# Attention heads of a graph-and-transformer kernel: another PSUM ring for the next pair's keys, longer pieces, and a fixed order on VectorE

## The chip, the cores and the metric

The kernel runs on one core of one Trainium2 chip. The metric is device time in microseconds (us) of one execution. A core has TensorE (PE in the profile; its weight loads are PEld), VectorE (DVE), ScalarE (ACT), GpSimd (POOL) and SyncE (SP), and 16 DMA engines. Each engine takes its own instructions in order and waits on semaphores for the others. Matrix products land in PSUM[...].

## The reference, cut to what matters

Everything is fp32. 1250 nodes with 768 features pass two graph attention layers, and then one transformer block: attention with 12 heads of 64, and a mixture of 8 experts. The change touches the attention of that block alone:

```python
qkv = (x @ Wqkv).reshape(B, T, 3, H, HD)
q, k, v = (qkv[:, :, 0], qkv[:, :, 1], qkv[:, :, 2])
scores = jnp.einsum('bqhd,bkhd->bhqk', q, k) * jnp.float32(HD) ** (-0.5)
attn = jax.nn.softmax(scores, axis=-1)
out = jnp.einsum('bhqk,bkhd->bqhd', attn, v).reshape(B, T, D)
```

with B = 1, T = 1250, H = 12, HD = 64.

## The kernel before

The heads are worked in six pairs (p), and the queries in three chunks of 417, 417 and 416 (k). One pair and chunk is a unit: 18 units, one after the other. The 1250 keys of a unit lie in ten tiles of 125 (j). Scores are held transposed, keys on the partitions and two heads beside each other, so that a tile is 125 x 834 (832 in the third chunk).

Work on a unit is spread over two rounds of the loop at line 737. While unit `u` has its weights and values computed, the scores of the unit after it, `nxt`, are computed.

- `scores(j)` (line 655) takes a tile `st` from the ring `pair_psum` (two buffers of two banks each), makes both heads' products (L659), copies them to `sT` on ScalarE (L662) and, from j = 1 on, takes the running maximum `most` over the tiles on VectorE (L668). For j = 1 the maximum reads the copy of tile 0 and `st` of tile 1.
- `top()` (L675, L677) transposes `most` into a `ptop` tile of the same ring and reduces it on VectorE to one maximum per query, `m`. `row()` (L684) spreads `m` over the partitions into the tile `mb`, which has one buffer.
- `weights(j)` subtracts `mb` from `sT` on VectorE (L689), takes the exponential on ScalarE (L690) and sums the tiles on GpSimd into `acc` (L695).
- `values(j)` multiplies the weights by the values into `pav` on PE (L703).
- `divide()` of the unit before turns `acc` into the sums `pz` on PE (L712), and takes the reciprocal (L718) and the product (L719) on VectorE.

Between these, PE makes the keys and queries of the next pair, `queries_keys` (line 607): a generator that yields after each product over 128 features. For each chunk there are six steps for the keys (`pk`) and six for the queries (`pq`); after the sixth ScalarE moves the result to `qk` (L625). `go(steps, n)` runs n steps. Twelve steps fall in each unit of the first five pairs; the sixth pair has no next one, so its three units have none. `pk` takes the buffer of `mb`; `pq` takes that of `pz`. The weights `wqk` are fetched by SP, once per pair, into a single buffer.

The order of instructions on PE is as the program writes it inside `tc.manual_schedule`. On the other engines a planner puts them in order by its own estimate of what is ready first. The loop of before, in short:

```python
go(steps, DC - 2)
if nxt is not None:
    nxt.scores(0)
u.row()
u.weights(0)
u.weights(1)
```

and then five double steps, each with two `scores`, two `weights` and two `values`, the first with one `scores`; two steps of the queries go into each of the first three.

Of the kernel before, what the change touches and what calls it, by code (L numbers as in the profile page):

```python
# [10 lines left out]
F32 = mybir.dt.float32  # L11
# [16 lines left out]
def gnn_ffn_kernel(  # L28
# [27 lines left out]
    P = 128  # L56
    T = 125
    NT = N // T
# [101 lines left out]
    with tc.tile_pool(name="cnt", bufs=1) as cpool:  # L160
# [52 lines left out]
        with tc.tile_pool(name="edge", bufs=1) as ep, \  # L213
# [54 lines left out]
            def find_rows():  # L268
                nc.vector.tensor_scalar(begun, nodes, head, None, ALU.is_gt)
                pk = epc.tile([P, 512], F32, tag="pc", name="pk")  # L270
                for t in range(NT):
                    nc.tensor.matmul(pk[:T, t:t + 1], begun[:, t * T:(t + 1) * T], oneb,
                                     start=True, stop=True)
                return pk
# [56 lines left out]
            with tc.manual_schedule(engines=fixed):  # L331
                pk = find_rows()
# [64 lines left out]
            with tc.manual_schedule(engines={mybir.EngineType.PE, mybir.EngineType.DVE}):  # L397
                for g in range(NP // PG):
# [11 lines left out]
                    u, q0 = divmod(g * PG, T)  # L410
# [175 lines left out]
    with tc.tile_pool(name="att", bufs=2) as ap, \  # L586
# [8 lines left out]
        def pair_psum(name):  # L595
            return aps.tile([P, 2, 512], F32, tag="s", name=name)
# [10 lines left out]
        def queries_keys(p):  # L607

            wqk = ap.tile([P, DC, 2, P], F32, tag="wqk", name="wqk", bufs=1)
            for i in (1, 0):  # L610
                nc.sync.dma_start(wqk[:, :, i, :], Wqkv[:, i * D + p * P:i * D + (p + 1) * P].rearrange(
                    "(c p) f -> p c f", p=P))
            qk = ap.tile([P, 2, N], F32, tag="qk", name="qk")
            yield qk
            for c0, w in CHUNKS:
                for i in (1, 0):
                    if i == 1:
                        pq = apm.tile([P, 2, 512], F32, tag="mb", name="pk")[:, 0, :]
                    else:
                        pq = apa.tile([P, 512], F32, tag="pz", name="pq")  # L620
                    for c in range(DC):
                        nc.tensor.matmul(pq[:, :w], wqk[:, c, i, :], yT[:, c, c0:c0 + w],  # L622
                                         start=(c == 0), stop=(c == DC - 1))
                        if c == DC - 1:
                            nc.scalar.mul(qk[:, i, c0:c0 + w], pq[:, :w], 1.0 if i == 1 else HD ** -0.5)  # L625
                        yield None

        def go(steps, n):
            for _ in range(n if steps is not None else 0):
                next(steps, None)  # L630
# [15 lines left out]
        class Unit:  # L646
# [67 lines left out]
            def divide(self):  # L714
# [4 lines left out]
                nc.vector.tensor_tensor(aT[:, self.p, self.c0:self.c0 + w], self.pav[:, :w], rz[:, :w], ALU.mult)  # L719

        steps = queries_keys(0)
        qks = [next(steps)]
        wp = load_big_weight(Wproj, "wp")
        BEFORE = 2
        with tc.manual_schedule(engines={mybir.EngineType.PE}):
# [4 lines left out]
            u = Unit(0, 0, qks[0])  # L730
# [5 lines left out]
        steps = last = None  # L736
        for n, (p, k) in enumerate(units):
            if k == 0:
                steps = None
                if p + 1 < DC:  # L740
                    steps = queries_keys(p + 1)
                    qks.append(next(steps))
            nxt = Unit(*units[n + 1], qks[units[n + 1][0]]) if n + 1 < len(units) else None
            u.ns = NT if nxt is not None else NS
            with tc.manual_schedule(engines={mybir.EngineType.PE}):

                go(steps, 2)
                u.top()
                if last is not None:
                    last.divide()  # L750
                go(steps, DC - 2)
                if nxt is not None:
                    nxt.scores(0)
                u.row()
                u.weights(0)
                u.weights(1)
                for j in range(0, NT, 2):
                    for i in range(2):
                        if nxt is not None and j + i > 0:
                            nxt.scores(j + i)  # L760
                    if j < 6:
                        go(steps, 2)
                    for i in range(2):
                        if j + i + 2 < NT:
                            u.weights(j + i + 2)
                    for i in range(2):
                        u.values(j + i)
            last, u = u, nxt
# [305 lines left out]
```

## Time and profile before

| what | value |
|---|---|
| median of 3 runs | 1541.51 us (1534.36 to 1543.46) |
| the profiled execution | 1542.12 us |
| its span, first to last instruction | 1540.3 us |
| first unit's first `ptop` to that of unit 17 | 691.4 to 1176.8 us |
| PE busy over the span | 1454.5 us (94%) |
| VectorE busy over the span | 797.8 us (52%) |
| ScalarE busy over the span | 597.6 us (39%) |

In a group line of the profile stand the line, the engine, the operation, the tiles written and read, the shapes and the count; then the busy time and the mean duration in ns of one; then the idle time of the engine before these instructions and what ended most of it. In a timeline line stand the start, the length, the engine, the line and operation, and in brackets the idle time before and its releaser. A product of fp32 appears as two matmuls in the count, so `st` of one tile is four (two heads).

### The profile page before, as it was taken

How to read it: one execution, taken by the hardware profiler on the slowest of the kernel's cores; microseconds unless marked ns; L12 is line 12 of the kernel's file. 1: busy time of each engine (PE TensorE's matmuls, PEld its weight loads, DVE VectorE, ACT ScalarE, POOL GpSimd, SP SyncE). 2: the span in 40 equal slices, each digit the busy share in tenths (PEclk: the TensorE clock that was granted, in tenths of full speed). 3: DMA queues.
4: the chain of work that ended last, by engine and by line, in shares of the span. 5: the costliest groups of instructions: out<-in, count | busy, mean ns of one | idle time of the engine just before them, and what ended most of it. 6: DMA issues, size and time to landing. Idle time of an engine off the chain costs nothing.

```text
span 1540.3 us, 15938 instructions
## 1 busy us (share of the span) xinstructions
PE 1454.5 (94%) x5981; PEld 782.3 (51%) x5981; DVE 797.8 (52%) x1285; ACT 597.6 (39%) x950; POOL 431.6 (28%) x287
## 2 busy tenths in 40 slices
PE   3889999999999999999999999999988997799998
PEld 2476655555555555553344444434333665466665
DVE  4698633205326740117877877877888665011111
ACT  3321503202414621215655655655656354212121
POOL 5300000000000002004764664664666222122222
PEclk9956999999999999999999999999999997899999
DMA  6200010000021118940000000000030333755644
GB/s 182 66 1 32 11 72 0 0 11 2 1 81 55 56 44 339 407 176 20 1 21 1 21 0 21 1 21 1 0 101 1 131 119 113 288 169 179 219 153 142
DMA packets 48847, 125.49 MB, mean 81 GB/s; under 512 B 6103, under 2 KB 22680, under 8 KB 48768
## 3 DMA queue, kind: packets, MB, share of 16 engines
q1 hardware_dynamic: 30540, 55.04, 10.8%
q0 software_dynamic: 12688, 57.10, 9.8%
q10 hardware_dynamic: 5540, 12.31, 2.7%
q8 instruction: 48, 0.79, 0.2%
q14 instruction: 31, 0.25, 0.1%
HBM read 71.30 MB, written 57.60 MB: 84 GB/s over the span
## 4 chain that ended last, share of the span: by engine, by line
PE 71%; DVE 9%; issue 8%; DMA 5%; ACT 4%; POOL 2%; POOLq 0%; SPq 0%; ACTq 0%; DVEq 0%
PE pagg L525 12%; PE ph L201 9%; PE st L659 8%; PE pav L703 7%; PE pk L622 5%; PE pv L638 5%; PE phe L988 5%; PE poe L997 5%; PE pq L622 4%; DMA xd<-yn,slot 2%; DVE sT L689 2%; PE pc L409 2%; PE pe L190 2%; PE po L846 2%; PE ptr L140 1%
## 5 line engine op out<-in xcount | busy, mean ns | idle before, releaser
L695 POOL TENSOR_TENSOR acc<-acc,sT 125x834 f32<-125x834 f32 (+1 forms) x139 | 272.9, 1963 | 10.9
L525 PE MATMUL pagg<-h,wt 125*125 125x385 f32 (+1 forms) x800 | 262.7, 486 | 0.4 <-DVE wt L518 0.4
L668 DVE TENSOR_TENSOR most<-most,st 125x834 f32<-125x834 f32 (+1 forms) x144 | 147.0, 1021 | 105.3 <-ACT sT L662 101.9
L525 PEld LDWEIGHTS pagg<-h,wt 125*125 125x125 f32 x800 | 147.5, 187 | 106.0 <-DVE wt L518 2.7
L689 DVE TENSOR_TENSOR sT<-sT,mb 125x834 f32<-125x834 f32 (+1 forms) x180 | 174.1, 1016 | 22.9 <-PE mb L684 22.9
L690 ACT ACTIVATE sT<-sT 125x834 f32<-125x834 f32 (+1 forms) x180 | 158.4, 900 | 49.8 <-DVE sT L689 49.4
L662 ACT COPY sT<-st 125x834 f32<-125x834 f32 (+1 forms) x180 | 151.5, 847 | 51.4 <-PE st L659 46.4
L659 PE MATMUL st<-qk 64*125 64x417 f32 (+1 forms) x720 | 164.5, 556 | 3.9 <-DVE most L668 3.8
L703 PE MATMUL pav<-sT,v 125*64 125x417 f32 (+1 forms) x720 | 151.1, 532 | 9.3 <-ACT sT L690 9.3
L600 POOL MEMSET zero<- 128x772 f32 x1 | 0.7, 741 | 519.2 <-PE ptr L140 519.2
L695 POOL TENSOR_TENSOR acc<-sT 125x834 f32<-125x834 f32 (+1 forms) x18 | 35.3, 1963 | 276.0 <-ACT sT L690 276.0
L659 PEld LDWEIGHTS st<-qk 64*125 64x125 f32 x720 | 56.6, 184 | 99.1 <-DVE most L668 42.9
L703 PEld LDWEIGHTS pav<-sT,v 125*64 125x64 f32 x720 | 42.5, 136 | 106.0 <-issue 44.5
L997 PE MATMUL poe<-we,hT 128*128 128x384 f32 x264 | 88.8, 486 | 0.0
L622 PE MATMUL pq<-yT,wqk 128*128 128x417 f32 (+1 forms) x216 | 88.1, 534 | 0.0
L846 PE MATMUL po<-wp,aT 128*125 128x384 f32 x240 | 87.5, 498 | 0.0
L988 PE MATMUL phe<-xT,we 128*128 128x384 f32 (+1 forms) x288 | 86.6, 460 | 0.0
L1001 DVE SCALAR_TENSOR_TENSOR sofar<-poe,weight,sofar 128x768 f32<-128x768 f32 x25 | 25.4, 1018 | 116.3 <-PE poe L997 116.2
L622 PE MATMUL pk<-yT,wqk 128*128 128x417 f32 (+1 forms) x216 | 84.0, 526 | 0.0
L201 PE MATMUL ph<-gw,xnT 128*125 128x384 f32 x240 | 82.6, 504 | 0.0
L638 PE MATMUL pv<-wv,yT 128*125 128x384 f32 x240 | 79.9, 490 | 1.4 <-issue 1.4
L201 PE MATMUL ph<-gw,x1T 128*125 128x384 f32 x240 | 78.6, 487 | 0.0
(219 smaller groups left out, 1734.6 us busy)
## 6 DMA issues: line engine op xcount, KB each, us to landing
xd<-zero POOLq DMA_DIRECT2D x8, 3860.0 KB, 47.4
we<-in_L_ffn_W_dram SPq DMA_DIRECT2D x16, 1152.0 KB
xr<-xd SPq DMA_DIRECT2D x25, 386.0 KB
gw<-in_L_gnn_W_dram SPq DMA_DIRECT2D x2, 2304.0 KB
wqk<-in_L_ffn_Wqkv_dram SPq DMA_DIRECT2D x12, 384.0 KB
xres<-in_x_dram SPq DMA_DIRECT2D x10, 375.0 KB
xsd<-xres ACTq DMA_DIRECT2D x10, 375.0 KB
wv<-in_L_ffn_Wqkv_dram SPq DMA_DIRECT2D x1, 2304.0 KB
```

The lines of the kernel that those rows point to most:

```text
L201: nc.tensor.matmul(po[:, s, :DH], xT[:, c, t * T:(t + 1) * T], w[:, c, s * DH:(s + 1) * DH], start=(c == 0), stop=(c == DC - 1))
L525: nc.tensor.matmul(po[:, s, :DH + s], ws[j][:, (d - d0) * T:(d - d0 + 1) * T], h[:, j, s * DH:(s + 1) * DH + s], start=(j == 0), stop=(j = ...
L622: nc.tensor.matmul(pq[:, :w], wqk[:, c, i, :], yT[:, c, c0:c0 + w], start=(c == 0), stop=(c == DC - 1))
L638: nc.tensor.matmul(pv[:T, s, :DH], yT[:, c, t * T:(t + 1) * T], wv[:, c, s * DH:(s + 1) * DH], start=(c == 0), stop=(c == DC - 1))
L659: nc.tensor.matmul(st[:T, i, :w], self.qk[r, 1, j * T:(j + 1) * T], self.qk[r, 0, self.c0:self.c0 + w], start=True, stop=True)
L662: nc.scalar.copy(s[:, :, :w], st[:T, :, :w])
L689: nc.vector.tensor_tensor(s[:, :, :w], s[:, :, :w], self.mb[:T, :, :w], ALU.subtract)
L690: nc.scalar.activation(s[:, :, :w], s[:, :, :w], AF.Exp)
L695: nc.gpsimd.tensor_tensor(self.acc[:, :, :w], prev[:, :, :w], s[:, :, :w], ALU.add)
L703: nc.tensor.matmul(self.pav[r, :w], v[:, j, hd0:hd0 + HD], s[:, i, :w], start=(j == 0), stop=(j == NT - 1))
L988: nc.tensor.matmul(ph[:, :n * P], w1[:, c, f * P:(f + 1) * P], xT[:, c, :n * P], start=(c == 0), stop=(c == DC - 1))
L997: nc.tensor.matmul(po[:, d, :DH], hT[:, f, s * P:(s + 1) * P], w2[:, f, d * DH:(d + 1) * DH], start=(f == 0), stop=(f == FC - 1))
```

## The change

Three things. The keys' tile `pk` comes from the scores' ring `pair_psum`, and no longer from the buffer of `mb`. VectorE's instructions in the loop are kept in the order of the program, as PE's are. And the order of the loop is another: `scores(0)` moves from before `row()` into the first double step; three `weights` stand ahead of the double steps and not two, and run three tiles ahead of `values`; the queries' six steps come as four right after these and two in the second double step, and no longer as three times two.

```diff
                 for i in (1, 0):
                     if i == 1:
-                        pq = apm.tile([P, 2, 512], F32, tag="mb", name="pk")[:, 0, :]
+                        pq = pair_psum("pk")[:, 0, :]
                     else:
                         pq = apa.tile([P, 512], F32, tag="pz", name="pq")
...
-            with tc.manual_schedule(engines={mybir.EngineType.PE}):
+            with tc.manual_schedule(engines={mybir.EngineType.PE, mybir.EngineType.DVE}):
 
                 go(steps, 2)
                 u.top()
                 if last is not None:
                     last.divide()
                 go(steps, DC - 2)
-                if nxt is not None:
-                    nxt.scores(0)
                 u.row()
-                u.weights(0)
-                u.weights(1)
+                for j in range(3):
+                    u.weights(j)
+                go(steps, 4)
                 for j in range(0, NT, 2):
                     for i in range(2):
-                        if nxt is not None and j + i > 0:
+                        if nxt is not None:
                             nxt.scores(j + i)
-                    if j < 6:
+                    if j == 2:
                         go(steps, 2)
                     for i in range(2):
-                        if j + i + 2 < NT:
-                            u.weights(j + i + 2)
+                        if j + i + 3 < NT:
+                            u.weights(j + i + 3)
                     for i in range(2):
                         u.values(j + i)
```

`NT` is 10 and `DC` is 6.

## The prediction

> **What bounds the kernel now.** I read the page first, for the engines' shares and the groups of the attention loop (lines 646 to 719). Names from here on: in unit n, score j is `scores(j)` of the next unit on TensorE (PE), copy j and max j are its ScalarE copy and VectorE maximum, sub j and exp j are `weights(j)` of the unit itself on VectorE and ScalarE, and value j is `values(j)` on PE.
>
> ```profile
> PE 1454.5 (94%) x5981; PEld 782.3 (51%) x5981; DVE 797.8 (52%) x1285; ACT 597.6 (39%) x950; POOL 431.6 (28%) x287
> L668 DVE TENSOR_TENSOR most<-most,st 125x834 f32<-125x834 f32 (+1 forms) x144 | 147.0, 1021 | 105.3 <-ACT sT L662 101.9
> L689 DVE TENSOR_TENSOR sT<-sT,mb 125x834 f32<-125x834 f32 (+1 forms) x180 | 174.1, 1016 | 22.9 <-PE mb L684 22.9
> L690 ACT ACTIVATE sT<-sT 125x834 f32<-125x834 f32 (+1 forms) x180 | 158.4, 900 | 49.8 <-DVE sT L689 49.4
> L662 ACT COPY sT<-st 125x834 f32<-125x834 f32 (+1 forms) x180 | 151.5, 847 | 51.4 <-PE st L659 46.4
> ```
>
> The reader should see that a maximum waits for ScalarE's copy, not for PE. Next I asked for the busy time by stretch: from the first `ptop` of unit 0 to that of unit 15 (the fifteen units that also make keys and queries), and over the next two units, which make none.
>
> ```profile
> 691.42:1125.24 433.82, 427.05 (x1852) 174.92 (x1853) 337.66 (x328) 257.99 (x331) 264.48 (x135) 1.00 0.06 16
> 1125.24:1176.83 51.59, 43.26 (x201) 15.64 (x201) 44.97 (x44) 33.33 (x40) 35.17 (x19) 0.93 0.15 36
> ```
>
> The columns after the length are PE, PEld, DVE, ACT and POOL. A unit takes 433.82/15 = 28.92 us, with PE full and VectorE at 78%. Then the timeline of VectorE in one unit (its `pk` starts at 748.17, the next at 777.07):
>
> ```profile
> 750.73 1.20 DVE L677 TENSOR_REDUCE m<-ptop 105x8 f32<-105x1000 f32 x1 [1.83 <-PE ptop L675]
> 751.85 2.76 DVE L718 RECIPROCAL rz<-pz 128x417 f32<-128x417 f32 x1
> 754.64 0.59 DVE L719 TENSOR_TENSOR aT<-pav,rz 128x417 f32<-128x417 f32 x1
> 756.59 2.88 DVE L689 TENSOR_TENSOR sT<-sT,mb 125x832 f32<-125x832 f32 x3 [1.35 <-PE mb L684]
> 759.39 1.02 DVE L668 TENSOR_TENSOR most<-sT,st 125x834 f32<-125x834 f32 x1
> 760.32 2.88 DVE L689 TENSOR_TENSOR sT<-sT,mb 125x832 f32<-125x832 f32 x3
> 763.12 1.01 DVE L668 TENSOR_TENSOR most<-most,st 125x834 f32<-125x834 f32 x1
> 768.71 1.01 DVE L668 TENSOR_TENSOR most<-most,st 125x834 f32<-125x834 f32 x1
> 770.17 1.02 DVE L668 TENSOR_TENSOR most<-most,st 125x834 f32<-125x834 f32 x1 [0.45 <-ACT sT L662]
> 772.42 2.15 DVE L668 TENSOR_TENSOR most<-most,st 125x834 f32<-125x834 f32 x2 [1.23 <-ACT sT L662]
> 775.65 2.15 DVE L668 TENSOR_TENSOR most<-most,st 125x834 f32<-125x834 f32 x2 [1.08 <-ACT sT L662]
> ```
>
> The planner lets the subtractions run ahead: all ten are done by 768.8, and the last maxima follow the scores with VectorE partly idle. That is how PE stays fed. And the end of that unit, all engines:
>
> ```profile
> 773.70 1.90 PE L659 MATMUL st<-qk 64*125 64x417 f32 x8
> 774.63 0.30 PEld L659 LDWEIGHTS st<-qk 64*125 64x125 f32 x4 [0.64 <-DVE most L668]
> 774.77 1.79 ACT L662 COPY sT<-st 125x834 f32<-125x834 f32 x2 [1.59 <-PE st L659]
> 775.53 1.62 PE L703 MATMUL pav<-sT,v 125*64 125x416 f32 x8
> 777.07 1.67 PE L622 MATMUL pk<-yT,wqk 128*128 128x417 f32 x4
> ```
>
> From it come the lags: copy 1.07 after its score starts on PE, maximum 0.03 after the copy, next score 0.06 after the maximum that frees its slot.
>
> **What the Trainium skill says.** "PSUM — Partial Sum Buffer", section "PSUM bank collisions raise a hardware error": two engines may not read one bank at once, reads against reads included. The trace agrees: all 162 maxima start at least 32 ns after the copy of the same tile ended. So score, copy, maximum is a chain. "TensorEngine Tiling (Array Packing)", section "Key Properties": changing the tiling mode drains TensorE. Here a lone score takes 0.90 us to the next piece and a pair 1.59, so a change costs about 0.2. "Perfetto Trace Analysis", section "Tensor Engine Instruction (MATMUL, LD_WEIGHTS)", calls VectorE and ScalarE strict FIFO: with a fixed order, a maximum that waits holds every subtraction behind it.
>
> **The change part by part, PE.** Pieces of the unit, start to start in the timeline of before: `pk` 1.51, `ptop` 0.94, `pz` 0.86, `pk` 2.99, score 0.89, `mb` 1.05, score 0.90, then `pq` 1.59, 1.60, 1.60 (three of two steps), four pairs of scores at 1.59, 1.59, 1.69, 1.83, values 1.23 + 0.86 (parted by a wait of 0.31) and four pairs at 1.55: 28.9. After: `pk` 1.51, `ptop` 0.94, `pz` 0.86, `pk` 2.9, `mb` 1.0, `pq` 2.99 and 1.60, five score pairs at 1.59, five value pairs at 1.55: 27.5. If nothing waits, PE gains 1.4 us a unit, 21 us in 15 units.
>
> Putting `pk` into the scores' ring costs nothing by itself: its slot was score 8's, free when max 8 is done (0.8 us early in the table below; a later max 8 would hold `pk` by as much); `mb` no longer waits for the eviction of `pk`, which only the lone score 0 covered. `pq` moves up to follow `mb` and needs the reciprocal done, which by the timeline ends 6.44 after `pk` starts; `pq` would start at 7.28. The earlier end of `pq` lets SP issue the next weights some 3 us sooner; they were 8 us early already.
>
> **VectorE's order.** Time zero is the first `pk`. Reduction 2.56, reciprocal 3.68, product 6.48, as now. `mb` starts at 6.23 and lets sub 0 start 1.2 later: 7.43, 8.38, 9.33. Max 1 is next in the fixed order. Scores 0 and 1 come only after `pq`, at 10.27 and 10.97; copies 0 and 1 at 11.34 and 12.09, so max 1 starts at 12.97. VectorE stands still from 10.3 to 12.97 with sub 3 to 9 ready behind it; in before it ran straight from sub 2 into max 1 and on. Fifteen starts follow max 1. Eleven at the trace's 0.93 to 0.96 and four maximum after maximum at 1.13 make 14.8 to 15.1, and the last takes 1.02: max 9 ends at 28.9 if VectorE never waits again. `ptop` needs it 1.51 after the next `pk`, so a period of 27.4 is VectorE's own floor, as tight as PE's.
>
> It does wait, since max j and score j+2 now follow each other in turn. I take ScalarE in order of readiness (copies 0.85, exponentials 0.90, starts 0.1 closer). Double step 1: scores at 13.41 and 14.11, max 2 and 3 at 15.82 and 16.91 (copy 3 stood behind exp 3), sub 5 and 6 at 17.86 and 18.81. Step 2: scores 18.14, copy 4 behind exp 5, max 4 at 20.60 and max 5 at 22.15 (waits 0.84 and 0.49), sub 7 and 8 to 25.0. Step 3: scores 6 and 7 wait for those maxima, 21.68 and 23.23; value 7 waits for exp 7 until 25.11; max 6 and 7 at 25.00 and 26.06. Step 4: scores 8 and 9 at 26.08 and 27.14, sub 9 27.01, exp 9 28.06, value 9 at 29.02, next `pk` 29.89. PE's waits are 0.4, 0.85, 0.3, 0.1, 0.36 and 0.3, about 2.4 us: more than the 1.4 that the pieces save. The same arithmetic with the orders of before gives 28.87, against 28.92 in the trace.
>
> ScalarE's order is not given by the change, so I bound it. Exponentials put before copies that are ready at nearly the same time (the planner did this in before: exp 0 ahead of copy 1) delay maxima: with copy 3 behind exp 4 and copy 4 behind exp 5 the same table gives 30.7, with exp 3 ahead of copy 2 as well 31.7. Copies as early as useful give 29.4, strict program order 34.8. I take 30.3, between the first two. Fifteen units: 15 x 30.3 - 433.8 = +20.7. The two units without keys go from 25.8 to about 26.2, the last one loses at most 0.6: +1. The profiled execution took 1542.12 (span 1540.3); with +21.7 it would be 1563.8, and against the median of the runs, 0.6 lower, 1563.
>
> **The rivals.** First, the other side: VectorE's order costs nothing and PE's pieces pay, 27.5 a unit, 15 x 27.5 - 433.8 = -21, 1520. For it: VectorE's floor is 27.4 too. It decides where VectorE waits under 1.5 us in all after max 1 (28.92 less 27.4); above it PE has lost more than it won. Against: even the best order of ScalarE leaves 29.4. Second, a tie: the waits eat the gain, 28.4 to 29.4 a unit, 1534 to 1549; it needs shorter lags than I read. Third, ScalarE falls into program order, 33 to 34.8 a unit: 1603 to 1630. Against it: before, the planner served what was ready.
>
> **How the numbers follow.** Forecast (29.4 to 32 a unit, 1549 to 1588 with the median) 0.62, of which 0.10 lies within 1%; PE's floor 0.15; tie 0.15; program order 0.08. One per cent, 15 us, is about what a measurement of this kernel tells from no change. So faster 0.15, same 0.25, slower 0.60. The range, 1533 to 1602, leaves out the faster rival and nearly all of the last.
>
> **What would show it.** Right: periods between `ptop` groups of 29.4 to 31.7; VectorE idle some 2.7 us before the maximum that reads `sT`; idle of PEld before `st` put down to `most`, and before `pav` to exponentials, over 1 us a unit; `mb` with no wait for `qk`. Wrong: periods under 28.5, or maxima that start before the copy of their tile ended. If POOL's sum were late, `pz` would wait for `acc`; I have it 1 us early.

## The result and the profile after

The changed kernel takes 1569.81 us (median of 6 runs, 1567.70 to 1570.93) against 1541.86 (6 runs, the three of the table above among them): a ratio of 1.0182, 95% interval 1.0167 to 1.0197. It is slower by 28 us. The profiled execution has a span of 1569.2 us, 28.9 more than the 1540.3 of before.

First the page of the changed kernel, the same rows as were shown of before:

```profile
PE 1453.3 (93%) x5981; PEld 780.5 (50%) x5981; DVE 800.0 (51%) x1285; ACT 601.8 (38%) x950; POOL 431.5 (27%) x287
L668 DVE TENSOR_TENSOR most<-most,st 125x834 f32<-125x834 f32 (+1 forms) x144 | 147.1, 1022 | 113.3 <-ACT sT L662 112.2
L690 ACT ACTIVATE sT<-sT 125x834 f32<-125x834 f32 (+1 forms) x180 | 160.5, 900 | 74.6 <-DVE sT L689 71.7
L689 DVE TENSOR_TENSOR sT<-sT,mb 125x834 f32<-125x834 f32 (+1 forms) x180 | 175.2, 1017 | 6.6 <-PE mb L684 6.6
L662 ACT COPY sT<-st 125x834 f32<-125x834 f32 (+1 forms) x180 | 150.7, 848 | 56.4 <-PE st L659 54.6
```

No instruction is longer (a maximum takes 1022 ns against 1021, an exponential 900 in both), and every engine runs as many instructions as before. What has grown is idle time: of ScalarE before its exponentials (74.6 us against 49.8) and of VectorE before its maxima. The row of the maxima leaves out max 1, which reads `sT` and has a group of its own; the waits of all maxima, and those of PE's weight loads for a maximum, are these (us in total, times, the longest), first before, then after:

```profile
DVE most L668 <- ACT sT L662: 147.2, 60, 45.3
PEld st L659 <- DVE most L668: 42.9, 74, 1.5
```
```profile
DVE most L668 <- ACT sT L662: 194.6, 99, 45.3
PEld st L659 <- DVE most L668: 94.3, 102, 2.5
```

Of the 47 us that VectorE waits longer, 37 stand before max 1 (82.4 against 45.3). Then the two stretches, from the first `ptop` of unit 0 to that of unit 15, and over the two units without keys:

```profile
691.40:1152.17 460.77, 426.83 (x1853) 174.04 (x1852) 339.28 (x328) 262.12 (x331) 264.46 (x135) 1.00 0.06 18
1152.17:1205.20 53.03, 42.90 (x200) 14.96 (x200) 45.41 (x44) 33.18 (x40) 35.06 (x19) 0.97 0.02 7
```

The fifteen units take 460.77 us against 433.82, +26.95; the next two 53.03 against 51.59, +1.44; what follows takes 0.5 more. That is the whole 28.9. A unit went from 28.92 to 30.72 us. PE's idle time in the first stretch (length less PE) went from 6.8 to 33.9 us, +27.2: PE waits.

VectorE in a unit whose `pk` starts near 842.7, from the reduction on:

```profile
845.26 1.20 DVE L677 TENSOR_REDUCE m<-ptop 105x8 f32<-105x1000 f32 x1 [1.66 <-PE ptop L675]
...
850.02 2.88 DVE L689 TENSOR_TENSOR sT<-sT,mb 125x832 f32<-125x832 f32 x3 [0.26 <-PE mb L684]
855.38 1.02 DVE L668 TENSOR_TENSOR most<-sT,st 125x834 f32<-125x834 f32 x1 [2.47 <-ACT sT L662]
856.32 1.95 DVE L689 TENSOR_TENSOR sT<-sT,mb 125x832 f32<-125x832 f32 x2
858.18 1.02 DVE L668 TENSOR_TENSOR most<-most,st 125x834 f32<-125x834 f32 x1
860.10 1.02 DVE L668 TENSOR_TENSOR most<-most,st 125x834 f32<-125x834 f32 x1 [0.90 <-ACT sT L662]
861.03 1.95 DVE L689 TENSOR_TENSOR sT<-sT,mb 125x832 f32<-125x832 f32 x2
863.76 1.02 DVE L668 TENSOR_TENSOR most<-most,st 125x834 f32<-125x834 f32 x1 [0.78 <-ACT sT L662]
865.30 1.02 DVE L668 TENSOR_TENSOR most<-most,st 125x834 f32<-125x834 f32 x1 [0.52 <-ACT sT L662]
866.24 1.95 DVE L689 TENSOR_TENSOR sT<-sT,mb 125x832 f32<-125x832 f32 x2
...
869.90 1.03 DVE L668 TENSOR_TENSOR most<-most,st 125x834 f32<-125x834 f32 x1 [0.77 <-ACT sT L662]
870.84 1.02 DVE L689 TENSOR_TENSOR sT<-sT,mb 125x832 f32<-125x832 f32 x1
...
873.56 1.02 DVE L668 TENSOR_TENSOR most<-most,st 125x834 f32<-125x834 f32 x1 [0.77 <-ACT sT L662]
```

The hole of 2.47 us before max 1 is there, with ready subtractions behind it. After it VectorE waits again before max 3, 4, 5, 7 and 9, each time for a copy. The last subtraction, which before was over at 768.8 (20.6 after `pk`), now starts at 870.84 (28 after). ScalarE has put exp 3 and 4 ahead of copy 3, and exp 5 ahead of copy 4:

```profile
857.63 1.69 ACT L690 ACTIVATE sT<-sT 125x832 f32<-125x832 f32 x2
859.22 0.85 ACT L662 COPY sT<-st 125x834 f32<-125x834 f32 x1
...
862.09 0.90 ACT L690 ACTIVATE sT<-sT 125x832 f32<-125x832 f32 x1 [1.61 <-DVE sT L689]
862.89 0.84 ACT L662 COPY sT<-st 125x834 f32<-125x834 f32 x1
```

And what PE makes of it in the second half of that unit:

```profile
864.84 0.97 PE L659 MATMUL st<-qk 64*125 64x417 f32 x4 [0.88 <-DVE most L668]
866.38 0.97 PE L659 MATMUL st<-qk 64*125 64x417 f32 x4 [0.57 <-DVE most L668]
...
870.98 0.97 PE L659 MATMUL st<-qk 64*125 64x417 f32 x4 [0.83 <-DVE most L668]
871.88 1.88 PE L703 MATMUL pav<-sT,v 125*64 125x416 f32 x8
871.89 0.90 ACT L690 ACTIVATE sT<-sT 125x832 f32<-125x832 f32 x1 [0.78 <-DVE sT L689]
872.84 0.20 PEld L703 LDWEIGHTS pav<-sT,v 125*64 125x64 f32 x4 [0.77 <-ACT sT L690]
873.69 1.67 PE L622 MATMUL pk<-yT,wqk 128*128 128x417 f32 x4
```

Score 6 waits for max 4, score 7 for max 5, score 9 for max 7 and value 9 for exp 9, and only then comes the next `pk`.

### The profile page after: what moved, and what is told of

It is laid out like the page before. It is cut to its first block, busy times and chain, and to the rows that moved or that the text cites. A ratio compares the mean times of both kernels' runs of the same rounds, so it can differ in the third digit from the quotient of the medians.

```text
span 1569.2 us, 15910 instructions
## 1 busy us (share of the span) xinstructions
PE 1453.3 (93%) x5981; PEld 780.5 (50%) x5981; DVE 800.0 (51%) x1285; ACT 601.8 (38%) x950; POOL 431.5 (27%) x287
## 4 chain that ended last, share of the span: by engine, by line
PE 59%; DVE 14%; issue 8%; ACT 8%; DMA 6%; POOL 5%; POOLq 0%; SPq 0%; ACTq 0%; DVEq 0%
PE pagg L525 12%; PE ph L201 8%; PE pk L622 5%; PE pv L638 5%; PE phe L987 5%; PE poe L996 4%; POOL acc L695 4%; DVE sT L689 4%; PE pq L622 3%; ACT sT L690 3%; DVE most L668 3%; PE pav L703 3%; PE st L659 3%; ACT sT L662 3%; DMA xd<-yn,slot 2%
## 5 line engine op out<-in xcount | busy, mean ns | idle before, releaser
L668 DVE TENSOR_TENSOR most<-most,st 125x834 f32<-125x834 f32 (+1 forms) x144 | 147.1, 1022 | 113.3 <-ACT sT L662 112.2
L659 PE MATMUL st<-qk 64*125 64x417 f32 (+1 forms) x720 | 161.6, 548 | 33.9 <-DVE most L668 33.6
L690 ACT ACTIVATE sT<-sT 125x834 f32<-125x834 f32 (+1 forms) x180 | 160.5, 900 | 74.6 <-DVE sT L689 71.7
L703 PE MATMUL pav<-sT,v 125*64 125x417 f32 (+1 forms) x720 | 158.2, 537 | 6.7 <-ACT sT L690 4.9
L659 PEld LDWEIGHTS st<-qk 64*125 64x125 f32 x720 | 57.0, 182 | 136.9 <-DVE most L668 94.3
L703 PEld LDWEIGHTS pav<-sT,v 125*64 125x64 f32 x720 | 39.4, 136 | 113.6 <-ACT sT L690 59.5
L622 PE MATMUL pq<-yT,wqk 128*128 128x417 f32 (+1 forms) x216 | 82.8, 521 | 0.0
```

The lines of the kernel that those rows point to most:

```text
L659: nc.tensor.matmul(st[:T, i, :w], self.qk[r, 1, j * T:(j + 1) * T], self.qk[r, 0, self.c0:self.c0 + w], start=True, stop=True)
L668: nc.vector.tensor_tensor(self.most[:, :, :w], prev[:, :, :w], st[:T, :, :w], ALU.max)
L690: nc.scalar.activation(s[:, :, :w], s[:, :, :w], AF.Exp)
L703: nc.tensor.matmul(self.pav[r, :w], v[:, j, hd0:hd0 + HD], s[:, i, :w], start=(j == 0), stop=(j == NT - 1))
```

## The experiments

Theory A was the prediction's: VectorE, held to the program's order, goes in lockstep with the scores through the chain score, copy, maximum, next score, and everything else on VectorE and ScalarE stands behind its waits. The rivals: B, PE's new order is at fault (scores 0 and 1 come behind all the queries); C, the keys in the scores' ring. Below, "a unit" is the period between `ptop` groups in the middle of the fifteen units.

**Run e1: VectorE given back to the planner.** The changed kernel with

```diff
-with tc.manual_schedule(engines={mybir.EngineType.PE, mybir.EngineType.DVE}):
+with tc.manual_schedule(engines={mybir.EngineType.PE}):
```

> The changed kernel with VectorE's order given back to the planner; PE's new order and the new ring stay. Theory A (the fixed order on VectorE, in lockstep with the scores, is what costs): the planner lets all subtractions run ahead of max 2 again, and the unit falls from 30.8 us to 28.3 to 29.0 (my table of the unit with this kernel's order as built: 29.0), so 1533 to 1545 us, within 1% of before. Theory B (PE's new order, with scores 0 and 1 behind all the queries, is what costs): the unit stays above 30, 1560 us or more. Theory C (the keys in the scores' ring): also stays, 1560 or more.

Measured: 1539.05 us, 0.9986 of before (0.9973 to 0.9998), a unit of 28.7 us. The loss is gone with PE's order and the ring still in place, so B and C fall as its cause: neither costs it alone. VectorE's timeline of this run:

```profile
839.93 6.61 DVE L689 TENSOR_TENSOR sT<-sT,mb 125x832 f32<-125x832 f32 x7 [0.27 <-PE mb L684]
846.46 1.01 DVE L668 TENSOR_TENSOR most<-sT,st 125x834 f32<-125x834 f32 x1
...
853.52 2.15 DVE L668 TENSOR_TENSOR most<-most,st 125x834 f32<-125x834 f32 x2 [1.39 <-ACT sT L662]
```

Seven subtractions fill the place of the hole, and max 1 starts with no wait. What PE's longer pieces might have won isn't seen yet: only 0.2 us of the 1.4 a unit. (With VectorE the planner also reordered ScalarE; the last four runs keep the two apart.)

**Run e2: VectorE's order fixed in the kernel before,** and nothing else (the same edit the other way).

> The kernel before with VectorE's order fixed as the program writes it (two tiles ahead) and nothing else. Theory A: slower than before, and more than the changed kernel, since exponentials run two tiles ahead and not three; the table gives 32.7 us a unit with the order as built, so about 1590 to 1600 us. Theories B and C: as before, 1535 to 1547 us.

Measured: 1595.73 us, 1.036 (1.0325 to 1.0394), a unit of 32.5 us. The one edit alone costs 54 us, twice the whole change. So the rest of the change wins back part of it. The waits of this run:

```profile
DVE most L668 <- ACT sT L662: 204.3, 106, 45.9
```

against 147.2 us in 60 waits before.

**Run e3: the ring alone,** the first hunk of the change in the kernel before.

> The kernel before with the keys' tile taken from the scores' ring and nothing else. Theory A: no change, 28.9 us a unit, 1535 to 1547 us. Theory C: most of the 28 us, 1560 or more, with pk waiting for most.

Measured: 1541.15 us, 1.0003 (0.9991 to 1.0015). The ring costs nothing and brings nothing by itself. `mb` no longer waits for the eviction of `pk` (9.0 us in 15 waits before); `pk` waits for a maximum instead (10.9 us in 15).

**Run e4: six weights ahead, to fill the hole.** The changed kernel with

```diff
-for j in range(3):
+for j in range(6):
     u.weights(j)
...
-if j + i + 3 < NT:
-    u.weights(j + i + 3)
+if j + i + 6 < NT:
+    u.weights(j + i + 6)
```

> The changed kernel with six weights ahead of the double steps and not three, so that VectorE's hole before max 1 (2.5 us) is filled with subtractions 3 to 5, and the fixed order has only four among the maxima. If the hole alone is the loss (a simple form of theory A), the unit falls by about that, to 28.3 or less, 1535 us or less. If the loss is the chain of score, copy and maximum with what stands ahead of each on its engine, it does not: the planner now puts exponentials 3 to 5 ahead of copy 1 on ScalarE, max 1 is some 2.7 us later, and the table gives 31.2 us, 1565 to 1577 us. Theory B: above 30 us either way.

Measured: 1576.25 us, 1.0226 (1.0188 to 1.0265), a unit of 30.9 us in most of the fifteen: no better than the change. ScalarE and VectorE in one unit of this run:

```profile
853.75 2.76 ACT L690 ACTIVATE sT<-sT 125x832 f32<-125x832 f32 x3 [1.47 <-DVE sT L689]
856.41 0.85 ACT L662 COPY sT<-st 125x834 f32<-125x834 f32 x1
857.15 2.47 ACT L690 ACTIVATE sT<-sT 125x832 f32<-125x832 f32 x3
859.52 1.60 ACT L662 COPY sT<-st 125x834 f32<-125x834 f32 x2
```
```profile
852.69 5.68 DVE L689 TENSOR_TENSOR sT<-sT,mb 125x832 f32<-125x832 f32 x6 [0.26 <-PE mb L684]
860.40 1.02 DVE L668 TENSOR_TENSOR most<-sT,st 125x834 f32<-125x834 f32 x1 [2.03 <-ACT sT L662]
```

The planner put exponentials 3 to 5 ahead of copy 1. Max 1 starts 7.71 us after sub 0, against 5.36 in the changed kernel: the hole was filled and came back 2 us long, behind those exponentials. So subtractions put ahead don't shorten the unit when ScalarE's order changes with them. What the hole costs by itself this run doesn't tell; e8 and e6 say more.

**Run e5: ScalarE fixed too, in the program's order.** The changed kernel with `mybir.EngineType.Activation` added to the engines.

> The changed kernel with ScalarE's order fixed too, as the program writes it: each double step's two exponentials ahead of its two copies' maxima... that is, copies j and j+1 stand behind the exponentials of the double step before, which wait for subtractions behind the maxima. Theory A in its full form (the chain score, copy, maximum with all that stands ahead of each on its engine): my table gives 35.0 us a unit in this order, 33.9 for the two without keys, so 15 x 6.0 + 2 x 8 = 106 us above before, 1635 to 1655 us. If ScalarE's order were of no weight (VectorE alone decides): as the changed kernel, 1565 to 1575 us.

Measured: 1642.37 us, 1.0649 (1.0632 to 1.0667), a unit of 34.6 us, the two without keys 69.2 us together (forecast 67.8). ScalarE's timeline:

```profile
882.24 1.83 ACT L690 ACTIVATE sT<-sT 125x832 f32<-125x832 f32 x2 [1.98 <-DVE sT L689]
883.98 1.59 ACT L662 COPY sT<-st 125x834 f32<-125x834 f32 x2
887.96 1.83 ACT L690 ACTIVATE sT<-sT 125x832 f32<-125x832 f32 x2 [2.40 <-DVE sT L689]
889.70 1.59 ACT L662 COPY sT<-st 125x834 f32<-125x834 f32 x2
```

and VectorE's in the same stretch:

```profile
884.85 2.15 DVE L668 TENSOR_TENSOR most<-most,st 125x834 f32<-125x834 f32 x2 [1.71 <-ACT sT L662]
886.91 1.95 DVE L689 TENSOR_TENSOR sT<-sT,mb 125x832 f32<-125x832 f32 x2
```

The period of a double step is 5.7 us, and the two engines wait for each other in turn: ScalarE idles 2.4 us for VectorE's subtractions, which stand behind maxima, which wait 1.7 us for ScalarE's copies, which stand behind its exponentials.

**Run e8: ScalarE in the best order found, VectorE in lockstep.** The loop's `scores` and `weights` were parted into product, copy and maximum, and subtraction and exponential, and called from a list, which keeps PE's and VectorE's orders of the changed kernel:

```diff
+ORDER = ("s0 s1 e0 s2 e1 p0 p1 c0 v0 c1 v1 e2 m1 p2 s3 p3 "
+         "c2 s4 e3 m2 c3 e4 pq v2 m3 v3 s5 p4 s6 p5 c4 v4 "
+         "e5 m4 c5 v5 e6 m5 p6 s7 p7 c6 s8 v6 e7 c7 m6 v7 "
+         "e8 p8 m7 s9 c8 p9 m8 v8 e9 c9 v9 m9 ").split()
...
+for what in ORDER:
```

(s subtraction, e exponential, p product of scores, c copy, m maximum, v values, pq two steps of the queries; all three engines fixed.)

> The changed kernel's orders of PE and VectorE, with ScalarE fixed by hand in the best order that I found for them (e0 e1 c0 c1 e2 c2 e3 c3 e4, q, c4 e5 c5 and so on by turns). The prediction says that even this leaves 29.4 us a unit: 1543 to 1553 us, no faster than before. If ScalarE's order is the whole loss: PE's floor, 27.5 a unit, 1525 us or less.

Measured: 1544.21 us, 1.0018 (1.0011 to 1.0026), a unit of 29.1 us. From the changed kernel to this one nothing but ScalarE's order changes, so about 1.6 us a unit (30.7 less 29.1) are ScalarE's order under the lockstep. The hole before max 1 is as long as in the changed kernel:

```profile
875.78 1.02 DVE L680 TENSOR_TENSOR most<-sT,st 125x834 f32<-125x834 f32 x1 [2.47 <-ACT sT L672]
```

No order that I found for ScalarE brings this lockstep below the time of before. In the next run, with another order on VectorE as well, the remaining 1.5 us go too.

**Run e6: the same list with VectorE running ahead.** Only the list differs; ScalarE's order is that of e5 but for the queries' eviction, one place later.

```diff
+ORDER = ("s0 s1 e0 s2 e1 p0 s3 e2 p1 s4 c0 v0 c1 v1 e3 m1 "
+         "p2 e4 s5 p3 c2 s6 c3 m2 e5 pq v2 s7 e6 v3 m3 p4 "
+         "s8 p5 c4 v4 c5 m4 v5 e7 m5 p6 e8 s9 p7 c6 v6 m6 "
+         "c7 v7 e9 m7 p8 p9 c8 v8 c9 m8 v9 m9 ").split()
```

> PE's order of the changed kernel, with ScalarE nearly as in the run that fixes it in the program's order (e0 e1 e2 c0 c1 e3 e4 c2 c3 e5, q, e6 c4 c5 e7 e8 c6 c7 e9 c8 c9), and VectorE fixed by hand so that its subtractions run further ahead: s0 to s4, m1, s5 s6 m2 s7 m3 s8 m4 m5 s9, m6 to m9. Theory A: PE nearly reaches its own floor, 27.9 us a unit, so 15 us under before: 1523 to 1531 us. Theory B (scores 0 and 1 behind all the queries are too late on PE whatever VectorE does): no better than before, 1540 or more.

Measured: 1520.55 us, 0.986 (0.9837 to 0.9883), a unit of 27.6 us: faster than both kernels, and a little under the range expected (the table has 27.9). The fifteen units, and VectorE in one of them:

```profile
690.79:1103.90 413.11, 411.47 (x1853) 178.16 (x1852) 340.37 (x328) 258.12 (x331) 265.21 (x135) 1.00 0.06 19
```
```profile
861.60 4.76 DVE L701 TENSOR_TENSOR sT<-sT,mb 125x834 f32<-125x834 f32 x5 [0.28 <-PE mb L696]
866.96 1.02 DVE L680 TENSOR_TENSOR most<-sT,st 125x834 f32<-125x834 f32 x1 [0.60 <-ACT sT L672]
```

Five subtractions fill the place before max 1 but for 0.60 us. Max 1 comes no sooner than in the changed kernel, 5.36 us after sub 0 in both; but less is left for VectorE to do behind it, and PE is idle 1.6 us in 413. Against e5 the change is VectorE's order and almost nothing else: 34.6 to 27.6 us a unit. And B falls a second time: the matmuls of the fifteen units run in the order of the changed kernel, and PE reaches its floor.

**Run e7: the maximum ahead of the copy.** The changed kernel, lockstep and all, with the two readers of a score's bank in the other order in `scores`:

```diff
-s = ap.tile([T, 2, CW], F32, tag="sT", name="sT", bufs=15)
-nc.scalar.copy(s[:, :, :w], st[:T, :, :w])
-self.s.append(s)
 ...
     prev = self.s[0] if j == 1 else self.most
     nc.vector.tensor_tensor(self.most[:, :, :w], prev[:, :, :w], st[:T, :, :w], ALU.max)
+s = ap.tile([T, 2, CW], F32, tag="sT", name="sT", bufs=15)
+nc.scalar.copy(s[:, :, :w], st[:T, :, :w])
+self.s.append(s)
```

> The changed kernel with the maximum written ahead of the copy, so that VectorE reads a score's bank first and ScalarE's copy waits for it (j of 1 and up); VectorE's fixed order is the same lockstep, and the planner puts ScalarE in the program's order. If the loss is that VectorE in its fixed order waits for ScalarE's copies: the loop loses that link, 28.7 us a unit by my table with the orders as built, 1534 to 1546 us. If the loss is the lockstep alone, whatever releases the maximum: 30.5 and more, 1563 us or more.

Measured: 1529.83 us, 0.9915 (0.9896 to 0.9934), a unit of 28.5 us: under the range expected, though the table's 28.7 a unit was near (the first unit and the two without keys, which it doesn't cover, are shorter too). Its waits:

```profile
DVE most L665 <- PE st L659: 105.9, 28, 44.5
ACT sT L667 <- DVE most L665: 48.3, 94, 1.2
DVE most L665 <- ACT sT L667: 25.8, 15, 1.8
```

Only max 1, which reads copy 0, still waits for ScalarE. The wait for the bank, the part of PSUM that both read, has moved to the copy: in the changed kernel each of the 162 maxima starts 31 ns or more after the copy of its tile ended, and here each copy, from tile 1 on, 33 ns or more after the maximum ended. It costs less there; that behind a waiting copy stands less that PE needs soon is my reading, and was not tested by itself. VectorE's lockstep is the same as in the changed kernel, and in the fifteen units ScalarE's order is that of e5, instruction for instruction. So against e5 only the two readers changed places, and the unit fell from 34.6 to 28.5 us: what made the lockstep costly was that its maxima wait for ScalarE's copies.

The table that the prediction worked by hand, done again for each order that the planner made or the list fixed, against the trace, us a unit:

| kernel | table | measured |
|---|---|---|
| before | 29.0 | 28.9 |
| e1, VectorE free | 29.0 | 28.7 |
| e2, VectorE fixed alone | 32.7 | 32.5 |
| after, its two orders of ScalarE | 30.7 and 31.4 | 30.3 and 31.0 |
| e4, subtractions early | 31.2 | 30.9 |
| e5, ScalarE in program order | 35.0 | 34.6 |
| e8, ScalarE at its best | 29.4 | 29.1 |
| e7, maximum first | 28.7 | 28.5 |
| e6, VectorE ahead | 27.9 | 27.6 |

The entries of e1, e2 and e4 to e8 were on record before those runs; the others are for orders read from the traces (the prediction's own table for before has 28.87). The table is 0.1 to 0.4 too high throughout, and puts the kernels in the measured order but for the pair e1 and before, which it has equal.

## Why the prediction was right

Direction, place and range held. By its steps:

- **PE's pieces.** A floor of 27.5 us a unit was worked out; e6 runs at 27.6 with PE idle for 0.4% of the time. In the changed kernel the saving is real but lies under the waits.
- **The ring.** Nothing, as said (e3).
- **VectorE's hole.** Forecast 2.7 us, measured 2.47 in the trace. That filling it with subtractions may only move it, since the planner then moves ScalarE's exponentials, was not said in the prediction; e4 showed it.
- **The chain.** In the unit shown PE waits for max 4, 5 and 7 and for exp 7 and 9, as the table had it (score 8 also starts 0.06 us after max 6). Carried on to max 9, the prediction's table has about 2 us of waits of VectorE after max 1, 0.84 and 0.49 of them before max 4 and 5; in that unit they are 3.74. The 1.7 more stand before max 3 and max 7, whose copies came behind exp 4 and exp 8.
- **ScalarE's order.** The planner made the second of the orders that were bounded: exp 4 ahead of copy 3, exp 5 ahead of copy 4. In two chunks of three exp 8 stands ahead of copy 7 as well, which wasn't foreseen; these units take 31.0 us and the others 30.3. The bound for strict program order, 34.8, was measured as 34.6 (e5), and the best, 29.4, as 29.1 (e8).
- **The sum.** The mis-sized term is the 30.3 us taken between two orders: measured 30.72, so 15 x 0.42 = 6.3 us of the missing 7.2 (28.9 against a forecast of 21.7). The units without keys lost 1.44 and not 0.8, the rest about 0.5. That 30.3 came so near is in part luck. It lay between two bounds, 29.89 and 30.7, and two of three units ran in an order worse than either. For the orders that came the table gives 30.7 and 31.4, some 31.2 on average and 0.9 more than was taken; but the table is about 0.4 too high, and that took back half of the miss.
- **The rivals.** A gain would have needed VectorE's waits after max 1 under 1.5 us; they were 3.74, or 3.0 in the shorter units. That bound holds for the lockstep alone: e6 waits 1.8 us there at a period of 27.6, since its first five subtractions are over before max 1. The tie is where e8 lies; program order is where e5 lies.
- **The signs.** Periods, hole and the maxima behind their copies came as named, and the wait of `mb` for `qk` is gone. The sign at PEld, over 1 us a unit before `st` and before `pav`, could not tell the cases apart: the kernel before had it already, 42.9 and 42.2 us in all. The change took them to 94.3 and 59.5.

What isn't settled is why the planner places exp 8 ahead of copy 7 in some units; no run here shows it.

## What to carry to other kernels

A fixed order on an engine turns each wait of an instruction into a wait of all that stand behind it; before fixing one, lay the engine's instructions on the timeline of the others, and put ready work ahead of every instruction that waits for a chain through another engine. If two engines read the same PSUM bank, decide which goes first: with the same orders on all engines it was worth 34.6 against 28.5 us a unit here (e5 and e7). That the first should be the one whose queue holds the more urgent work is a guess from this one case. An engine that the planner still orders is part of the result, since fixing one engine changed the order on another, and a hole that is filled on the first may come back from the second.

## What the hardware showed beside

PE's busy time contains waits. The changed kernel and e6 run the same matmuls in the same order in the fifteen units (x1853 both), and the profile has PE busy for 426.83 us in one and 411.47 in the other. The granted clock is 1.00 in both. So 15 us of waiting count as busy in the changed kernel, and idle time alone understates what PE could gain. Before was 98% busy in that stretch and still had 20.7 us (433.82 less 413.11) to give, 15.6 of them out of busy time (427.05 less 411.47): waits in part, and in part the shorter pieces, which the profile doesn't tell apart.
